# One GpSimd combination moved behind its addition into S, and four VectorE operations per turn made two, in a four-layer modulated convolution

## The chip, the cores and the metric

The kernel runs on one core of a Trainium2 chip. The metric is the time of one execution in device microseconds (us); the kernel before has a median of 495.83 us in three runs (495.58 to 497.23).

## The reference

For 128 samples of 64 channels by 1024 positions, the reference adds to x the result of four convolution layers of three taps, each with weights of its own for each sample:

```python
def _layer(x, style, w, b, mw, mb, typ):
    s = style @ mw.T + mb
    weight = SCALE * w * s[:, None, :, None]
    demod = lax.rsqrt(jnp.sum(weight * weight, axis=(2, 3)) + EPS)
    weight = weight * demod[:, :, None, None]
    ...            # 'same', 'upsample' (with a blur), 'same', 'downsample' (with a blur)
out = x
for i, typ in enumerate(('same', 'upsample', 'same', 'downsample')):
    out = _layer(out, style, weights[i], biases[i], mod_w[i], mod_b[i], typ)
return x + out
```

Nothing in it is nonlinear, so a sample's four layers are one linear filter away from the ends of the sequence, and the few positions at the ends are computed on their own.

## The kernel before, in words

Four samples make a group q, so there are 32 groups (NQ = 32), two pairs of two samples each. For each group the kernel composes the filter from the layers' weights and then convolves x with it. All of it is in float32.

The weights of a group come from a chain of small matmuls on TensorE with 64 x 64 tiles. `scale3` scales the last layer's taps, `stage1_a` and `stage1_b` multiply them with the third layer's into PSUM psS, from where they come to the tile S; `stage2` multiplies S with the blur and the second layer into psR, and `stage3` with the first layer into psW and from there into Wf. In `stage1_b` VectorE writes two sums into S (L422), and then an addition (L425) puts a third part of S together: `t[:, :, 2] + t[:, :, 0]`. The first matmul of `stage2` (L439) reads that part.

The convolution is a fast one in the manner of Toom and Cook: x is split into three planes, five combinations T0 to T4 of the planes are multiplied with five combinations of the taps, and the products are recombined. The combinations go over an intermediate tile G (one buffer):

- `in_g01` (L555, recorded at L501): two planes of G from x, one VectorE operation for each pair of samples (128 x 688)
- `in_g2` (L560, recorded at L501): the third plane of G, both pairs in one operation
- `in1` (L565) and `in2` (L570): T1 and T2 from G, the sum and the difference of two planes, both pairs in one operation of 128 x 684, on GpSimd in nearly every turn
- `in04` (L577): T0 and T4 from G, one VectorE operation for each pair
- `in3` (L550): T3 from x, on VectorE

`conv0` to `conv4` (L590) are the products on TensorE, in PSUM psA, and for `conv4` in Y. `sum1` (y) and `sum2` (Y, then y at L641) are VectorE's recombinations between them; they have one input in PSUM. `combine_a` and `combine_b` (H, L501, and L498) are VectorE's combinations of the taps. ScalarE copies and scales what leaves PSUM and writes the output; SP issues the loads and stores.

The order on each engine is the order of the program text: there is no planner, each engine runs its own instructions in the order in which the loop issues them and waits on semaphores. Turn q of the loop convolves with group q, prepares n = q + 1 further, composes the weights of c = q + 2 and begins those of s = q + 3. It opens with `stage2(c)`, the Y sum of `sum2(q)` and `conv4(q)`, and closes with `conv2(n)`.

Eleven turns are slot turns (q = 1, 2, 3, 5, 6, 7, 9, 12, 14, 19, 24): they carry one more group of small matmuls (`slot`), for the ends of the sequence and for constants, at the place where the others call `stage1_a`. So in a slot turn `stage1_a` comes later, and `stage1_b` behind the first third of `conv2`. `extra(q, 0)` and `extra(q, 1)` stand near the end of a turn, behind `stage1_b`, and give some turns up to q = 25 a few small operations on VectorE, GpSimd or ScalarE.

In the kernel before, GpSimd runs `in1(c)` and `in2(c)` one behind the other in each turn from q = 1. In turns without a slot it then runs the addition of `stage1_b(s)`. In slot turns that addition is VectorE's, by the argument `nc_v`:

```python
        if q and c < NQ - 1:
            in1(c, nc_g)
            in2(c, nc_g)
        ...
        if q in SLOTS:
            stage1_a(s)
        elif s < NQ:
            stage1_b(s)
        ...
        if q in SLOTS:
            stage1_b(s, nc_v)
        extra(q, 0)
        extra(q, 1)
```

Of the kernel before, what the change touches and what calls it, by code (L numbers as in the profile page):

```python
# [50 lines left out]
ALU = mybir.AluOpType  # L51
# [12 lines left out]
def kernel(  # L64
# [12 lines left out]
    NQ = B // 4  # L77
# [5 lines left out]
    nc_v, nc_a, nc_g = nc.vector, nc.scalar, nc.gpsimd  # L83
# [42 lines left out]
    PL = NXC // 3  # L126
# [239 lines left out]
    def tap_matmul(ps, wd, at, n, weight, taps, first=False, last=False):  # L366
        for r, rows in enumerate(HALF):
            for c, cols in enumerate(HALF):
                nc.tensor.matmul(  # L369
                    ps[r][cols, at * C : (at + n) * C],  # L370
                    weight[rows],
                    wd[c if r == 0 else 1 - c][rows, taps],
                    start=first,
                    stop=last,
                    skip_group_check=True,
                )
# [34 lines left out]
            scaled_copy(nc_a, flat(st[r][:, :4]), ps[r][:, : 4 * C], tBn[:, q, r : r + 1])  # L411
        chain[q] = wd, ps, st, t

    def stage1_b(q, eng=nc_g):

        wd, ps, st, t = chain[q]
        tap_matmul(ps, wd, 1, 1, w2n[:, 3, :], slice(3, 4))
        tap_matmul(ps, wd, 3, 1, w2n[:, 4, :], slice(4, 5), last=True)
        for r in range(2):
            p1 = st[r][:, 0:1, :].to_broadcast([P, 2, C])  # L420
            sums = ps[r][:, C : 5 * C].rearrange("c (a b o) -> c a b o", a=2, b=2)[:, :, 0]
            nc_v.scalar_tensor_tensor(  # L422
                st[r][:, 4:, :], sums, tB[:, q, r : r + 1], p1, op0=ALU.mult, op1=ALU.subtract
            )
        eng.tensor_add(t[:, :, 2], t[:, :, 2], t[:, :, 0])  # L425
        chain[q] = st

    def stage2(q, pool=None, engs=(nc_a, nc_a), between=None):
# [71 lines left out]
    def sum_of(out, x, f, y, op=ALU.add):  # L500
        nc_v.scalar_tensor_tensor(out, x, f, y, op0=ALU.mult, op1=op)  # L501
# [23 lines left out]
    NJ = NB + 2  # L525
# [2 lines left out]
    A = {}  # L528
    SLOT = {0: ("T04", 0), 4: ("T04", 1), 1: ("T12", 0), 2: ("T12", 1), 3: ("T3", 0)}
    BOTH_PAIRS = slice(0, 2)  # L530

    def plane(buf, i, pairs=BOTH_PAIRS):

        at = PL * (2 - i) if i < 3 else PL * 2 + 1
        return buf[:, pairs, at : at + NJ]

    def t_tile(q, tag):
        if (q, tag) not in Ts:
            Ts[q, tag] = tpool.tile([P, 2, 1 + (tag != "T3"), PL], F32, tag=tag, name=f"{tag}_{q}")
        return Ts[q, tag]  # L540

    def g_tile(q):
        if q not in Gs:
            Gs[q] = gpool.tile([P, 2, 3 * PL], F32, tag="G", name=f"G{q}")
        return Xs[q % NX], Gs[q]

    def in3(q, pairs=BOTH_PAIRS):
        if q < NQ:
            X, t = Xs[q % NX], t_tile(q, "T3")
            nc_v.tensor_sub(t[:, pairs, 0, :NJ], plane(X, 3, pairs), plane(X, 1, pairs))  # L550

    def in_g01(q, c):
        if q < NQ:
            X, g = g_tile(q)
            sum_of(g[:, c, PL:], X[:, c, : 2 * PL], 0.5, X[:, c, PL:], ALU.subtract)  # L555

    def in_g2(q, pairs=BOTH_PAIRS):
        if q < NQ:
            X, g = g_tile(q)
            sum_of(plane(g, 2, pairs), plane(X, 3, pairs), 0.5, plane(X, 2, pairs), ALU.subtract)  # L560
# [6 lines left out]
    def in2(q, eng):  # L567
        if q < NQ:
            t, g = t_tile(q, "T12"), Gs[q]
            eng.tensor_sub(t[:, :, 1, :NJ], plane(g, 2), plane(g, 1))  # L570

    def in04(q, c):
        if q < NQ:
            t, g = t_tile(q, "T04"), Gs[q]
            a, b = g[:, c, :NJ], g[:, c, 2 * PL : 2 * PL + NJ]
            both = lambda v, step: bass.AP(v.tensor, v.offset, [list(v.ap[0]), [step, 2], [1, NJ]])
            nc_v.tensor_sub(t[:, c, :, :NJ], both(a, PL), both(b, 1))  # L577

    def product(q, m, ps, groups=range(K)):

# [43 lines left out]
    def conv1(q, *groups):  # L624
        product(q, 1, banks(q), groups or range(K))
# [106 lines left out]
    def const_of(l, bs):  # L732

        n = bs.stop - bs.start
        at = NB + 4 + l * n
        return Y[:, 0, at : at + n]
# [4 lines left out]
    def const_first(l, bs):  # L741
        src = c0f if l == 0 else cc[l - 1]
        for cols in HALF:
            nc.tensor.matmul(
                const_of(l, bs)[cols],
                wsum[T, l, :],
                src[T, bs],
                start=False,
                stop=True,
                skip_group_check=True,  # L750
            )
# [218 lines left out]
    var_newton(PART[0])  # L970
    for of in (table_C, vector_c0, table_3, vector_a1, vector_Da, vector_b1, vector_c2):
        of(PART[0])
    in_g01(0, 0)
    in3(0)
    stage2(0, None, BOTH)
    psL = unit(ps_conv, "psL")
# [1 line left out]
    nc_a.copy(raw[0][:, 0, :n_later], psL[0][:, :n_later])  # L978
    zeros_to_y(2, 456)
    const_first(0, PART[0])  # L980
    in_g01(0, 1)
    in_g2(0)
    load(NX)
    split_weights()
# [10 lines left out]
    conv3(0)  # L995
    copy_m3(0)
    const_first(1, PART[0])
    in04(0, 0)
    in04(0, 1)
    const_rest(1, PART[0], const_of(1, PART[0]))  # L1000
    stage3(1, 0)
    mod_by_layer(LATER, raw[0][:, 0], sc, AF.Identity)
    in3(1)
    conv1(0)
    in_g01(1, 0)
    in_g01(1, 1)
    const_first(2, PART[0])
    sum1(0)
    const_rest(2, PART[0], const_of(2, PART[0]))
# [15 lines left out]
    n, n1 = (bs.stop - bs.start for bs in (REST, PART[1]))  # L1025
# [75 lines left out]
    for q in range(NQ):  # L1101
        n, c, s = q + 1, q + 2, q + 3
        if q == 1:
            nc.sync.dma_start(Xe, x_ends)
        if q == 5:
            zeros()
        if n == NQ:
            conv4(q)
            for i in range(2):
                output(q, 2, i)  # L1110
            for i in range(2):
                output(q, 1, i, nc_v)
            for i in range(2):
                store(q, i, slice(1, 3))
            conv0(q, *range(K))
            for i, (eng, queue) in enumerate(zip(BOTH, (nc_a, nc.sync))):
                output(q, 0, i, eng)
                store(q, i, slice(0, 1), queue)
            break
        if c < NQ:  # L1120
            stage2(c)
        if n < NQ - 1:
            sum2(q)
        if n < NQ - 1:
            combine_a(n)
            combine_b(n)

        if n == NQ - 1:

            conv3(n, ps_w)  # L1130
            copy_m3(n)
            conv4(q, 0, 1)
            for i in range(2):
                output(q, 1, i)
            conv1(n)
            sum1(n)
            conv4(q, 2)
            for i in range(2):
                output(q, 2, i)
            in04(n, 0)  # L1140
            in04(n, 1)
            conv0(q, 0)
            conv2(n)
            conv0(q, 1, 2)
            sum2(n)
            for i in range(2):
                output(q, 0, i)
                store(q, i)
            continue

        conv4(q)
        if q == 0:
            var_matmul(PART[1], var_of(PART[1]), start=False)
            var_root(PART[1], var_of(PART[1]))
            var_inverse(PART[1])
            var_newton(PART[1])
            table_A(PART[1], dm[:, 2, PART[1]])
            for of in (table_C, vector_c0, table_3, vector_Da):
                of(PART[1])
        for i in range(2):  # L1160
            output(q, 2, i)
        if c < NQ:
            stage3(c, 0)
        conv3(n)
        copy_m3(n)
        in04(n, 0)
        in04(n, 1)
        if q:
            in3(c)
            in_g01(c, 0)  # L1170
            in_g01(c, 1)
        if c < NQ:
            stage3(c, 1)
        conv0(q, 0)
        conv1(n, 0)
        if q in SLOTS:
            slot(*SLOTS[q])
        elif s < NQ:
            stage1_a(s)
        conv1(n, 1, 2)  # L1180
        for i in range(2):
            output(q, 1, i)
        if q:
            in_g2(c)
            load(c + NX)
        if q and c < NQ - 1:
            in1(c, nc_g)
            in2(c, nc_g)
        if n == NQ - 2:
            combine_a(n + 1, lambda: sum1(n))  # L1190
            combine_b(n + 1)
        else:
            sum1(n)
        if q == 0:
            in_g01(c, 0)
            in_g01(c, 1)
        conv0(q, 1)
        if q in SLOTS:
            stage1_a(s)
        elif s < NQ:  # L1200
            stage1_b(s)
        conv0(q, 2)
        for i in range(2):
            output(q, 0, i)
        conv2(n, 0)
        if q in SLOTS:
            stage1_b(s, nc_v)
        extra(q, 0)
        extra(q, 1)
        if s + 1 < NQ:  # L1210
            scale3(s + 1)
        conv2(n, 1, 2)
        if n == NQ - 2:
            sum2(n)
            in1(n + 1, nc_v)
            in2(n + 1, nc_v)
        if q == 0:
            in_g2(c)
            in3(c)
            load(c + NX)  # L1220
            in1(c, nc_g)
            in2(c, nc_g)
        for i in range(2):
            store(q, i)
# [74 lines left out]
```

## Time and profile before

| | |
|---|---|
| median of three runs | 495.83 us |
| the profiled execution's own time | 496.51 us |
| its span in the profile | 494.7 us |
| granted TensorE clock | 0.997 |
| VectorE steps for G (L501) | 96, of 866 ns |
| VectorE steps for T0 and T4 (L577) | 64, of 865 ns |
| GpSimd steps in1, in2 (L565, L570) | 30 of each, of 1669 and 1666 ns |
| additions into S (L425) | 18 on GpSimd, 11 on VectorE |

The profile names an engine PE (matmuls), PEld (weight loads, which run beside the matmuls), DVE (VectorE), ACT (ScalarE) or POOL (GpSimd). A row of the view of groups has the line, the engine, the operation, what is written from what, the count, and then the busy time, the mean length of one and the idle time of the engine ahead of it. A row of the waits has who waited for whom, the time in total, how often and the longest. A row of the timeline has the start and the length in us, both counted from the span's start, and in brackets the idle time ahead of it and who ended it. Rows of the timeline merge equal neighbours (x2, x24), and the window that was asked for cuts them off. One turn of the loop goes from one first load of psR to the next.

### The profile page before, as it was taken

The numbers are of one execution on the slowest core, as the hardware profiler recorded it, in microseconds if no ns is written. First come the engines' busy times: TensorE is split into PE (matmuls) and PEld (weight loads), VectorE is DVE, ScalarE is ACT, GpSimd is POOL, SyncE is SP. The second block draws the span as 40 slices with busy tenths as digits, with TensorE's granted clock in tenths as the row PEclk, the third lists the DMA queues.
The fourth block names the chain that finished last, engine by engine and source line by source line (L and its number), as shares of the span: only waits on it lengthen the run. The fifth ranks groups of instructions, "written<-read, shape, count | busy, mean of one in ns | idle before, by whom it ended". The sixth has DMA issues, their size and how long they took to land.

```text
span 494.7 us, 22227 instructions
## 1 busy us (share of the span) xinstructions
PE 481.8 (97%) x10056; PEld 355.1 (72%) x10056; DVE 398.7 (81%) x704; ACT 290.5 (59%) x579; POOL 137.0 (28%) x164
## 2 busy tenths in 40 slices
PE   8999999999999999999999999999999999999994
PEld 6877687767777766767777777766766777777752
DVE  4986888798898869997768897759998768878783
ACT  5456646556565656556566556656555657566552
POOL 3544412344213223121223112223123323211200
PEclk9999999999999999999999999999999999999998
DMA  7220744443334442344443334442344442434224
GB/s 248 94 90 4 237 155 168 173 167 113 109 133 173 174 171 93 102 158 170 173 154 108 114 145 173 174 164 75 115 166 173 173 173 89 160 128 161 89 86 170
DMA packets 19727, 70.42 MB, mean 142 GB/s; under 512 B 2224, under 2 KB 2992, under 8 KB 19632
## 3 DMA queue, kind: packets, MB, share of 16 engines
q1 hardware_dynamic: 19408, 68.70, 39.0%
q8 instruction: 79, 1.29, 1.0%
q10 hardware_dynamic: 224, 0.29, 0.2%
q14 instruction: 16, 0.13, 0.1%
HBM read 35.36 MB, written 33.62 MB: 139 GB/s over the span
## 4 chain that ended last, share of the span: by engine, by line
PE 82%; DVE 11%; POOL 4%; issue 2%; ACT 1%; POOLq 0%; DVEq 0%
PE psA L590 37%; PE psR L439 14%; PE psW L480 13%; PE Y L590 9%; PE psS L369 5%; DVE G L501 3%; PE psE L820 2%; DVE H L501 2%; POOL T L565 1%; DVE T L577 1%; POOL T L570 1%; PE Y L169 1%; DVE Y L501 1%; DVE y L641 1%; DVE Wf L498 1%
## 5 line engine op out<-in xcount | busy, mean ns | idle before, releaser
L590 PE MATMUL psA<-T,H 64*64 64x340 f32 x2304 | 192.2, 446 | 0.7 <-DVE y L501 0.7
L565 POOL TENSOR_TENSOR T<-G 128x684 f32<-128x684 f32 x30 | 50.1, 1669 | 306.7 <-DVE G L501 266.6
L590 PEld LDWEIGHTS psA<-T,H 64*64 64x64 f32 x2304 | 92.8, 133 | 53.0 <-issue 6.7
L439 PE MATMUL psR<-S,E 64*64 64x192 f32 (+1 forms) x2304 | 88.0, 301 | 3.6 <-POOL S L425 2.3
L439 PEld LDWEIGHTS psR<-S,E 64*64 64x64 f32 x2304 | 77.3, 133 | 18.0 <-POOL S L425 7.6
L340 ACT ACTIVATE R<-psR,tC 128x448 f32<-128x448 f32 x63 | 36.6, 631 | 75.7 <-PE psR L439 73.9
L501 DVE SCALAR_TENSOR_TENSOR G<-X 128x688 f32<-128x688 f32 (+1 forms) x96 | 78.1, 866 | 0.0
L590 PE MATMUL psA<-T,Wf 64*64 64x340 f32 x768 | 74.0, 447 | 0.0
L501 DVE SCALAR_TENSOR_TENSOR y<-psA,m 128x680 f32<-128x680 f32 (+1 forms) x33 | 27.8, 845 | 46.8 <-PE psA L590 46.6
L340 ACT ACTIVATE Wf<-psW,t 128x384 f32<-128x384 f32 (+1 forms) x126 | 56.4, 498 | 11.5 <-PE psW L480 11.5
L480 PE MATMUL psW<-R,w0s 64*64 64x128 f32 (+1 forms) x1536 | 62.1, 287 | 0.4 <-ACT Wf L340 0.3
L590 PE MATMUL Y<-T,Wf 64*64 64x340 f32 x768 | 61.6, 446 | 0.4 <-DVE Y L501 0.3
L480 PEld LDWEIGHTS psW<-R,w0s 64*64 64x64 f32 x1536 | 51.1, 133 | 8.2 <-ACT Wf L340 1.2
L577 DVE TENSOR_TENSOR T<-G 128x684 f32<-128x684 f32 x64 | 52.7, 865 | 0.0
L659 ACT ACTIVATE o<-Y,tb,td 128x340 f32<-128x340 f32 x64 | 37.2, 631 | 23.4 <-ACT R L340 16.8
L570 POOL TENSOR_TENSOR T<-G 128x684 f32<-128x684 f32 x30 | 50.0, 1666 | 0.0
L369 PEld LDWEIGHTS psS<-wd,w2n 64*64 64x64 f32 x1160 | 38.5, 133 | 11.1
L659 ACT ACTIVATE o<-psA,tb,td 128x340 f32<-128x340 f32 x63 | 36.7, 634 | 14.9 <-PE psA L590 14.9
L590 PEld LDWEIGHTS Y<-T,Wf 64*64 64x64 f32 x768 | 31.8, 133 | 17.0 <-DVE Y L501 1.0
L340 ACT ACTIVATE S<-psS,tBn 128x256 f32<-128x256 f32 x58 | 24.4, 471 | 25.4 <-PE psS L369 25.3
L622 ACT COPY m<-psA 128x680 f32<-128x680 f32 (+1 forms) x33 | 23.3, 710 | 25.4 <-PE psA L590 25.4
L659 ACT ACTIVATE o<-y,tb,td 128x340 f32<-128x340 f32 x62 | 38.1, 668 | 0.0
(148 smaller groups left out, 529.2 us busy)
## 6 DMA issues: line engine op xcount, KB each, us to landing
X<-in_x SPq DMA_DIRECT2D x64, 516.0 KB, 4.5
out<-o SPq DMA_DIRECT2D x62, 510.0 KB, 4.4
out<-o SPq DMA_DIRECT2D x2, 340.0 KB, 4.4
Xe<-in_x_ends SPq DMA_DIRECT2D x1, 512.0 KB, 7.4
par<-in_params SPq DMA_DIRECT2D x2, 192.0 KB, 3.5
par_s<-in_params_s SPq DMA_DIRECT2D x1, 196.0 KB, 2.8
par<-in_params SPq DMA_DIRECT2D x2, 96.0 KB, 2.9
out<-Oe SPq DMA_DIRECT2D x1, 192.0 KB, 1.9
```

What stands on the lines that cost most here:

```text
L340: nc_a.activation(dst, src, AF.Copy, scale=f)
L369: nc.tensor.matmul(ps[r][cols, at * C : (at + n) * C], weight[rows], wd[c if r == 0 else 1 - c][rows, taps], start=first, stop=last, skip_ ...
L439: nc.tensor.matmul(ps[r][cols, lo * C : (lo + m) * C], E[rows, e + 2, :], src[rows, a, :], start=(n == 0), stop=(n == 8), skip_group_check ...
L480: nc.tensor.matmul(ps[r][cols, at : at + m * C], w0s[kind][rows, k, :], rt[c][rows, first : first + K * (m - 1) + 1 : K, :], start=(n == 1 ...
L501: nc_v.scalar_tensor_tensor(out, x, f, y, op0=ALU.mult, op1=op)
L565: eng.tensor_add(t[:, :, 0, :NJ], plane(g, 2), plane(g, 1))
L570: eng.tensor_sub(t[:, :, 1, :NJ], plane(g, 2), plane(g, 1))
L577: nc_v.tensor_sub(t[:, c, :, :NJ], both(a, PL), both(b, 1))
L590: nc.tensor.matmul(ps[s][cols, :NB], w, Ts[q, tag][rows, c, i, g : g + NB], start=(g == 0 and m == 3), stop=(g == K - 1), skip_group_check ...
L622: nc_a.copy(m3c[q][:, s], a)
L659: nc_a.activation(dst, src, AF.Identity, bias=add, scale=d3)
L820: nc.tensor.matmul(ps[r][cols, : HB * n].rearrange("c (b j) -> c b j", j=n), weight(i, r, c)[rows], moving(i, r, c)[rows], start=(i == 0), ...
```

## The change

Three things are different. In every turn from q = 1, in2 is issued behind `stage1_b`, so that GpSimd has in1, the addition into S, and then in2. `stage1_b` has lost its engine argument, so the addition of the eleven slot turns is GpSimd's, too. And `in_g01` and `in04` take a slice of pairs: within the loop, both pairs go in one VectorE operation, as they did for `in_g2` and `in3`; for the first groups and for the last one the pairs stay apart.

```diff
-    def stage1_b(q, eng=nc_g):
+    def stage1_b(q):
...
-        eng.tensor_add(t[:, :, 2], t[:, :, 2], t[:, :, 0])
+        nc_g.tensor_add(t[:, :, 2], t[:, :, 2], t[:, :, 0])
...
+    PAIR = slice(0, 1), slice(1, 2)
...
-    def in_g01(q, c):
+    def in_g01(q, pairs=BOTH_PAIRS):
         if q < NQ:
             X, g = g_tile(q)
-            sum_of(g[:, c, PL:], X[:, c, : 2 * PL], 0.5, X[:, c, PL:], ALU.subtract)
+            sum_of(g[:, pairs, PL:], X[:, pairs, : 2 * PL], 0.5, X[:, pairs, PL:], ALU.subtract)
...
-    def in04(q, c):
+    def in04(q, pairs=BOTH_PAIRS):
         if q < NQ:
             t, g = t_tile(q, "T04"), Gs[q]
-            a, b = g[:, c, :NJ], g[:, c, 2 * PL : 2 * PL + NJ]
-            both = lambda v, step: bass.AP(v.tensor, v.offset, [list(v.ap[0]), [step, 2], [1, NJ]])
-            nc_v.tensor_sub(t[:, c, :, :NJ], both(a, PL), both(b, 1))
+            a, b = g[:, pairs, :NJ], g[:, pairs, 2 * PL : 2 * PL + NJ]
+            both = lambda v, step: bass.AP(
+                v.tensor, v.offset, [*(list(d) for d in v.ap[:-1]), [step, 2], [1, NJ]]
+            )
+            nc_v.tensor_sub(t[:, pairs, :, :NJ], both(a, PL), both(b, 1))
...
-        in04(n, 0)
-        in04(n, 1)
+        in04(n)
         if q:
             in3(c)
-            in_g01(c, 0)
-            in_g01(c, 1)
+            in_g01(c)
...
-        if q and c < NQ - 1:
+        later = q and c < NQ - 1
+        if later:
             in1(c, nc_g)
-            in2(c, nc_g)
...
         if q in SLOTS:
-            stage1_b(s, nc_v)
+            stage1_b(s)
+        if later:
+            in2(c, nc_g)
         extra(q, 0)
         extra(q, 1)
```

More of the change, by code (lines that the diff above doesn't have):

```diff
@@ L972 @@
         of(PART[0])
-    in_g01(0, 0)
+    in_g01(0, PAIR[0])
     in3(0)
@@ L980 @@
     const_first(0, PART[0])
-    in_g01(0, 1)
+    in_g01(0, PAIR[1])
     in_g2(0)
@@ L997 @@
     const_first(1, PART[0])
-    in04(0, 0)
-    in04(0, 1)
+    in04(0)
     const_rest(1, PART[0], const_of(1, PART[0]))
@@ L1004 @@
     conv1(0)
-    in_g01(1, 0)
-    in_g01(1, 1)
+    in_g01(1, PAIR[0])
+    in_g01(1, PAIR[1])
     const_first(2, PART[0])
@@ L1139 @@
                 output(q, 2, i)
-            in04(n, 0)
-            in04(n, 1)
+            in04(n, PAIR[0])
+            in04(n, PAIR[1])
             conv0(q, 0)
@@ L1165 @@
         copy_m3(n)
-        in04(n, 0)
-        in04(n, 1)
+        in04(n)
         if q:
             in3(c)
-            in_g01(c, 0)
-            in_g01(c, 1)
+            in_g01(c)
         if c < NQ:
@@ L1194 @@
         if q == 0:
-            in_g01(c, 0)
-            in_g01(c, 1)
+            in_g01(c)
         conv0(q, 1)
```

## The prediction

> **What bounds the kernel now.** I read the page's busy shares first, then the waits, then the timeline around each start of psR, the first matmul group of a loop turn.
>
> ```profile
> PE 481.8 (97%) x10056; PEld 355.1 (72%) x10056; DVE 398.7 (81%) x704; ACT 290.5 (59%) x579; POOL 137.0 (28%) x164
> ```
>
> TensorE is the bound. So VectorE work that vanishes is worth something only in turns where TensorE waits for it. Which waits does TensorE have?
>
> ```profile
> PEld psR L439 <- POOL S L425: 7.6, 11, 1.3
> ...
> PE psR L439 <- POOL S L425: 2.3, 4, 0.7
> ```
>
> Inside the loop they stand almost all at psR, which needs GpSimd's addition into S: eleven waits of the weight loads, 7.6 us, of which 2.3 us in four turns (q=4, 10, 20, 21) reach the matmuls. An ordinary turn, q=26 into 27:
>
> ```profile
> 431.07 0.87 DVE L501 SCALAR_TENSOR_TENSOR y<-psA,m 128x680 f32<-128x680 f32 x1 [1.56 <-PE psA L590]
> 431.31 1.65 POOL L570 TENSOR_TENSOR T<-G 128x684 f32<-128x684 f32 x1
> ...
> 431.86 0.60 DVE L422 SCALAR_TENSOR_TENSOR S<-psS,tB,S 128x128 f32<-128x128 f32 x2
> ...
> 432.92 0.45 POOL L425 TENSOR_TENSOR S<-S 128x128 f32<-128x128 f32 x1
> ...
> 433.55 2.64 PEld L439 LDWEIGHTS psR<-S,E 64*64 64x64 f32 x72
> ```
>
> S is ready on VectorE at 432.46, but the addition starts at 432.92, when in2 (L570) leaves GpSimd; it ends at 433.37 and psR starts at 433.55. Here nothing is lost. One of the four bad turns, q=10:
>
> ```profile
> 195.25 1.65 POOL L570 TENSOR_TENSOR T<-G 128x684 f32<-128x684 f32 x1
> 195.30 2.01 DVE L835 TENSOR_TENSOR Ye<-raw,a 128x384 f32<-128x384 f32 x1
> ...
> 196.85 0.77 POOL L425 TENSOR_TENSOR S<-S 128x128 f32<-128x128 f32 x1
> ...
> 197.67 0.21 PEld L439 LDWEIGHTS psR<-S,E 64*64 64x64 f32 x8 [1.31 <-POOL S L425]
> ```
>
> in2 is late, so the addition is late (it ends at 197.62) and psR starts 0.05 behind it. A second thing is to be seen: L835, 384 elements from SBUF and SBUF, takes 2.01 us beside in2, and the addition 0.77 instead of 0.45 beside L835. In the slot turn q=9, with GpSimd idle, the same L835 takes 0.56:
>
> ```profile
> 182.97 0.56 DVE L835 TENSOR_TENSOR Ye<-raw,a 128x384 f32<-128x384 f32 x1
> 183.56 0.56 DVE L836 TENSOR_TENSOR Ye<-Ye,c 128x384 f32<-128x384 f32 x1
> 184.03 0.86 DVE L501 SCALAR_TENSOR_TENSOR Y<-m,psA 128x680 f32<-128x680 f32 x1
> ```
>
> So a VectorE step with its inputs in SBUF and a GpSimd step exclude each other: L835 stood about 1.45 us, until in2 was done. The Trainium skill, "SBUF — State Buffer", section "SBUF: two separate sides", says that the two share a port pair under an exclusive lock, held for the whole instruction by whichever starts first. The trace agrees (0.56 against 2.01 us), and by that rule a long in2 hurts wherever such steps meet it.
>
> **The change part by part.** *In2 behind the addition, turns without a slot.* The addition then waits for S and in1 alone. S is ready 1.1 us before psR in the ordinary turn (432.46 to 433.55), so nothing is gained there. In the four bad turns the wait goes; at most 2.3 us of matmul time, or, were each load wait to count in full, 7.6. I take the lower, since in the slot turn below psR's loads wait 0.48 us and no idle time stands at its matmuls. Of these 2.3 I count 1.2. What is late next is VectorE: these turns have extra steps between S and the Y sum (L501, Y<-m,psA), in2 now stands in their middle instead of at their head, and conv4, whose loads follow psR's 2.64 us of loads at once, needs Y. For q=20 three such steps are left and I count nothing; for q=4 and 10 0.3 each; for q=21, whose two steps fit around the addition, 0.6.
>
> *The addition of the slot turns, from VectorE to GpSimd.* There are eleven (q = 1, 2, 3, 5, 6, 7, 9, 12, 14, 19, 24), and in each psR hangs directly on this addition. q=9:
>
> ```profile
> 181.63 0.61 DVE L422 SCALAR_TENSOR_TENSOR S<-psS,tB,S 128x128 f32<-128x128 f32 x2 [1.61 <-PE psS L369]
> ...
> 182.16 0.28 DVE L425 TENSOR_TENSOR S<-S 128x128 f32<-128x128 f32 x1
> ...
> 182.55 0.17 PEld L439 LDWEIGHTS psR<-S,E 64*64 64x64 f32 x3 [0.48 <-issue]
> ```
>
> S ends at 182.24, psR starts at 182.55: 0.31 us. On GpSimd there come the hand-over, the addition and the way to psR. The hand-over is read from in1, which starts at 429.69 when the third G step ends at 429.52:
>
> ```profile
> 427.08 2.44 DVE L501 SCALAR_TENSOR_TENSOR G<-X 128x688 f32<-128x688 f32 x3
> ...
> 429.69 1.66 POOL L565 TENSOR_TENSOR T<-G 128x684 f32<-128x684 f32 x1 [10.26 <-DVE G L501]
> ```
>
> That is 0.17 us. The addition's durations on both engines:
>
> ```profile
> L425 POOL TENSOR_TENSOR S<-S x18: 447/517/975, 43.8 to 461.1; 128x128 f32<-128x128 f32 x18
> L425 DVE TENSOR_TENSOR S<-S x11: 279/281/944, 62.1 to 405.1; 128x128 f32<-128x128 f32 x11
> ```
>
> 0.17 + 0.45 + 0.05 is 0.67 against 0.31: 0.36 us later, eleven times 4.0. Corrections, estimates from the spread of these two rows and the lengths of the steps beside them: the one addition of 0.94 us on VectorE (q=1, beside in2) gets better by 0.7 against that, q=5 and q=7, which now lose 0.15 and 0.27 to in2, too; q=7 and q=19 have a step of 0.7 at the head of their extras, which the addition must let pass (0.3 each), q=12 and 14 one of 0.4 (0.1 each). Sum 3.6 us. Bounds: 0 if something hides it (I see no cover: psR is the next group in TensorE's order), and 11 × (0.975 − 0.279 + 0.22) = 10 if each addition met a VectorE step.
>
> The addition on GpSimd now waits for S, and in2 is queued behind it, then the small tables of the extras. Conv2, which reads in2's result, stands at the end of the next turn, and the next G steps, which overwrite its input, start no more than 6.5 us ahead of the next psR (427.08 to 433.55), half a turn after in2 is over; the tables are read later still, and no DMA is issued from this queue. So I cost the later in2 at nothing on this side; if a slot turn's addition were late by half a turn, G would wait, and in1 and S behind it.
>
> *In2 beside VectorE's extras in slot turns.* Until now in2 was long over when these ran. Now it starts when the addition ends, about 0.65 us behind S, and holds 1.65 us. Y and y read PSUM and don't meet it: in the ordinary turn y ran 0.87 us with most of it beside in2, and its 680 elements cost no more than a G step's 688. But extras that are not done by then stand still, and Y is queued behind them. I let the engines take turns: one extra step before the addition, one before in2. Two extras get through (q=1, 5, 12, 14, 19, 24), more don't. q=6 has six:
>
> ```profile
> 136.81 0.28 DVE L425 TENSOR_TENSOR S<-S 128x128 f32<-128x128 f32 x1
> ...
> 137.59 0.26 DVE L238 SCALAR_TENSOR_TENSOR dm<-nw,dm 128x96 f32<-128x96 f32 x1
> ...
> 139.03 0.86 DVE L501 SCALAR_TENSOR_TENSOR Y<-m,psA 128x680 f32<-128x680 f32 x1
> ...
> 139.94 0.21 PEld L590 LDWEIGHTS Y<-T,Wf 64*64 64x64 f32 x8 [0.33 <-DVE Y L501]
> ```
>
> L236, as short as L238, moves to 136.81, where the addition was; the addition runs to 137.5, L237 to 137.7, in2 to 139.35, the other four (1.44 us, from 137.59 to 139.03) to 140.8. Y comes 1.76 later, and conv4 already waits for it: 1.4 us on top of psR's 0.36. q=9: its copies get through, in2 runs from 183.0 to 184.65, L835 and L836 are left (1.06, from 182.97 to 184.03) and perhaps a copy, Y starts at 185.8 instead of 184.03; conv4, due 2.64 behind psR at 185.19, now has 0.3 to spare on a Y that ends at 184.89: 1.1 on top. q=3 waits already:
>
> ```profile
> 95.66 0.21 PEld L590 LDWEIGHTS Y<-T,Wf 64*64 64x64 f32 x8 [0.66 <-DVE Y L501]
> ```
>
> Its reciprocal runs beside the addition, the rest stands: about 1.0. q=2 and q=7, with one short step left: 0.2 each. Sum 3.9; bounds 0 (VectorE wins the pair each time) and 5 × 1.65 = 8.
>
> *One operation for both pairs.* Some thirty turns lose two starts of a VectorE step.
>
> ```profile
> L501 DVE SCALAR_TENSOR_TENSOR G<-X 128x688 f32<-128x688 f32 (+1 forms) x96 | 78.1, 866 | 0.0
> ```
>
> Against the addition on VectorE (128 elements, 0.279) 560 elements more cost 0.587 us, so 688 alone are 0.72 us. In the row of three G steps above a further one costs (2.44 − 0.866) / 2 = 0.787. One start less is thus worth 0.07 us (bounds 0 and 0.866 − 0.72 = 0.15), 0.14 per turn, if the longer operation keeps its rate; the G step and the T0/T4 step (L577) of the two pairs write separate places as before. It counts where VectorE sets the pace, and I take four turns: −0.6, with bounds of 0 and 30 × 0.3 = 9. Elsewhere, as in the ordinary turn, VectorE stands idle 1.56 us ahead of y until TensorE is done with psA, and an earlier G step only lengthens that.
>
> **Sum.** +3.6 + 3.9 − 1.2 − 0.6 = +5.7 on the profiled execution's 496.51 us (of which 494.7 is the span): 502.2. That execution lies 0.68 above the median of 495.83; by the median it is 501.5.
>
> **The rivals.** *The lock costs nothing.* If VectorE gets its short steps through ahead of in2, what is left is 3.6 − 2.3 − 0.6 = +0.7: 496.5. For it: steps of 0.2 us find gaps easily. Against it: L835's 2.01.
>
> *Faster: the load waits count in full.* If psR's loads set TensorE's pace, then all 7.6 us come back at the eleven psR of turns without a slot, the slots lose 4.0, the merges give 0.6, and with no lock the time is 495.83 − 7.6 + 4.0 − 0.6 = 491.6. It decides from the point where a load wait under 0.5 us costs matmul time. For it: the loads' row of waits is three times that of the matmuls. Against it: 0.48 us of load wait without idle matmuls in q=9, and the lock would take its 3.9 back, which leaves 495.5.
>
> *The lock takes more.* in2 could also reach the H steps in each slot turn (it ends about 1.6 us behind psR, and H starts there): 0.3 in each of ten, and G and in1 after them: 502.2 + 3 = 505.2, by the median 504.5. Conv3 needs the H sums later, so I don't take it.
>
> **How the numbers follow.** Forecast as above, 498 to 504.5: 0.64. Lock without cost, 494.5 to 497: 0.12. Faster by the load waits, 491 to 494.3: 0.14. More than 504.5: 0.10. About 0.3% (1.5 us) is what a measurement here tells from no change. Slower 0.74, within 0.12, faster 0.14. Range 495.0 to 505.0, which leaves most of the fast rival out and a little above; the forecast's own range is 498 to 504.5.
>
> **What would show it.** Right: in slot turns psR about 0.67 us behind S, with "POOL S L425" as releaser; VectorE's extras stretched by about 1.65 us in q=3, 6, 9, and conv4 waiting for Y there; in turns without a slot the addition ahead of in2 and no wait at psR; merged steps near 0.279 + 1248 × 0.00105 = 1.59 us. Wrong: no longer waits for Y, or ordinary turns shorter than now from psR to psR, which would mean that the load waits counted.

## The result, and the profile after

The changed kernel takes 494.2 us, median of 15 runs (493.27 to 495.95); the kernel before, run beside it, 495.88 (495.18 to 497.23). The ratio is 0.9961, with an interval from 0.9951 to 0.9971: faster by 1.9 us by the ratio, by 1.7 between the medians. The forecast was 501.5 with a range from 495.0, so both its sign and its range were wrong. The profiled execution took 494.43 us with a span of 492.6, against 496.51 and 494.7 before. The lines of the code move: in1 is now L566, in2 L571, the T0/T4 step L580, the product L593, while L422, L425 and L439 keep their numbers.

The page of the changed kernel, busy shares and two of its groups:

```profile
PE 480.1 (97%) x10056; PEld 363.4 (74%) x10056; DVE 406.0 (82%) x632; ACT 290.3 (59%) x579; POOL 141.9 (29%) x175
...
L571 POOL TENSOR_TENSOR T<-G 128x684 f32<-128x684 f32 x30 | 53.2, 1775 | 0.0
L580 DVE TENSOR_TENSOR T<-G 128x1368 f32<-128x1368 f32 (+1 forms) x33 | 50.5, 1534 | 0.0
```

VectorE has 72 instructions fewer and is 7.3 us *busier* (398.7 to 406.0): "busy" holds the time in which it stands behind GpSimd (with the merged operations alone, in e1 below, it is 392.5). in2 too has become longer (1.775 us in the mean, 1.666 before). TensorE does the same 10056 matmuls in a shorter span. Now the waits of the changed kernel (total, times, longest):

```profile
POOL S L425 <- ACT S L340: 20.3, 11, 4.0
...
PEld Y L593 <- DVE Y L501: 6.0, 9, 1.1
...
PE Y L593 <- DVE Y L501: 2.8, 5, 0.8
```

The row "psR L439 <- POOL S L425" of before, 7.6 us of load waits, is gone altogether, in the slot turns too, where the prediction expected it to appear. At conv4 nine waits for Y have grown out of two; five of them reach the matmuls as idle time (2.8 us). The row at the top names the mistake: eleven times, in q=0 and in ten of the eleven slot turns (in q=1 in1 is late), GpSimd sat idle until **ScalarE** (L340) released the addition. The view of L425's own instructions says the same, and lists nobody who waits for them:

```profile
L425 POOL TENSOR_TENSOR S<-S x29: 448/459/474, 43.8 to 457.8; 128x128 f32<-128x128 f32 x29
its engine sat idle before it (us, times) until:
  ACT S L340: 20.3, 11
who waited for it (us, times):
```

The slot turn q=9 after, whose stretch of before stands in the prediction:

```profile
180.12 0.84 ACT L340 ACTIVATE S<-psS,tBn 128x256 f32<-128x256 f32 x2 [0.28 <-PE psS L369]
...
181.04 0.46 POOL L425 TENSOR_TENSOR S<-S 128x128 f32<-128x128 f32 x1 [2.52 <-ACT S L340]
...
181.46 1.65 POOL L571 TENSOR_TENSOR T<-G 128x684 f32<-128x684 f32 x1
...
181.58 0.61 DVE L422 SCALAR_TENSOR_TENSOR S<-psS,tB,S 128x128 f32<-128x128 f32 x2 [1.61 <-PE psS L369]
...
182.11 1.05 DVE L816 COPY a<-Da 64x64 f32<-64x64 f32 x1
182.15 2.62 PEld L439 LDWEIGHTS psR<-S,E 64*64 64x64 f32 x72
...
184.65 0.86 DVE L501 SCALAR_TENSOR_TENSOR Y<-m,psA 128x680 f32<-128x680 f32 x1
...
185.56 0.49 PEld L593 LDWEIGHTS Y<-T,Wf 64*64 64x64 f32 x12 [0.80 <-DVE Y L501]
```

The addition starts at 181.04, 0.08 us after ScalarE's two copies are done (180.12 to 180.96), and is over at 181.50, before VectorE's two sums (L422) have even begun. psR follows at 182.15 with no wait, a moment before the sums are through (182.19): its first matmuls read parts 1 to 3, and only the next ones the sums. In the kernel before, the addition stood behind these sums in VectorE's queue and psR came at 182.55. Measured from the start of the sums, psR started 0.92 us behind it before and 0.57 now.

The code says why. L411 lets ScalarE write parts 0 to 3 of S (`flat(st[r][:, :4])`). L425 adds part 0 to part 2 and reads nothing else. VectorE's sums at L422 write parts 4 and 5 (`st[r][:, 4:, :]`). So the addition never depended on the sums. In the kernel before it was late by the order of a queue alone: behind the sums on VectorE in slot turns, behind in2 on GpSimd in the others.

Where did the time go? From start and end of every matmul record I worked out how much later each group of the loop began than it could have (its idle time and 0.2 us, by which groups that wait for nothing overlap in the records). A loss at psR or conv4 is put down to the turn q whose addition or extras it waits for; both groups open turn q + 1. Summed over the loop, in the two profiled executions:

| us lost ahead of | before | after |
|---|---|---|
| psR, turns without a slot | 3.7 | 0 |
| psR, slot turns | 2.3 | 0 |
| conv4's first group (waits for Y) | 1.0 | 4.9 |
| other groups of the loop | 1.7 | 2.7 (0.73 of it one gap without a releaser) |

6.0 us come back at psR and 3.9 are handed over to conv4, the next group that needs a late engine. The 2.1 that are left fit the result. But the other groups lost 1.0 more in this execution, so the whole table falls by 1.1 only, and the loop, from the psR that opens q=0 to the one that opens q=29, is 1.4 us shorter (430.7 to 429.3). The same kernel profiled again (e14 below) lacks the gap of 0.73 us, and its loop is 1.8 shorter (428.9). A single profile is no better than that.

### The profile page after: what moved, and what is told of

Its sections match the earlier page's. It is cut to its first block, busy times and chain, and to the rows that moved or that the text cites. A ratio compares the mean times of both kernels' runs of the same rounds, so it can differ in the third digit from the quotient of the medians.

```text
span 492.6 us, 22188 instructions
## 1 busy us (share of the span) xinstructions
PE 480.1 (97%) x10056; PEld 363.4 (74%) x10056; DVE 406.0 (82%) x632; ACT 290.3 (59%) x579; POOL 141.9 (29%) x175
## 4 chain that ended last, share of the span: by engine, by line
PE 86%; DVE 9%; POOL 1%; issue 1%; ACT 1%; DVEq 0%
PE psA L593 40%; PE psW L480 14%; PE psR L439 12%; PE Y L593 11%; PE psS L369 5%; PE psE L823 2%; DVE Y L501 1%; DVE G L501 1%; PE Y L169 1%; DVE S L422 1%; ACT o L662 1%; DVE Ve L839 1%; PE Y L316 1%; DVE Ye L839 0%; DVE Ve L838 0%
## 5 line engine op out<-in xcount | busy, mean ns | idle before, releaser
L593 PE MATMUL psA<-T,H 64*64 64x340 f32 x2304 | 193.3, 446 | 0.6 <-DVE y L501 0.5
L593 PEld LDWEIGHTS psA<-T,H 64*64 64x64 f32 x2304 | 95.3, 133 | 51.1 <-issue 7.6
L566 POOL TENSOR_TENSOR T<-G 128x684 f32<-128x684 f32 x30 | 50.1, 1671 | 283.4 <-DVE G L501 251.5
L439 PE MATMUL psR<-S,E 64*64 64x192 f32 (+1 forms) x2304 | 87.6, 299 | 0.7 <-ACT S L340 0.4
L439 PEld LDWEIGHTS psR<-S,E 64*64 64x64 f32 x2304 | 80.8, 133 | 8.2 <-issue 1.0
L340 ACT ACTIVATE R<-psR,tC 128x448 f32<-128x448 f32 x63 | 36.6, 631 | 69.2 <-PE psR L439 67.4
L501 DVE SCALAR_TENSOR_TENSOR G<-X 128x1376 f32<-128x1376 f32 (+2 forms) x66 | 76.1, 1191 | 0.0
L593 PE MATMUL psA<-T,Wf 64*64 64x340 f32 x768 | 74.8, 447 | 0.0
L593 PE MATMUL Y<-T,Wf 64*64 64x340 f32 x768 | 62.2, 448 | 3.1 <-DVE Y L501 2.8
L340 ACT ACTIVATE Wf<-psW,t 128x384 f32<-128x384 f32 (+1 forms) x126 | 56.4, 498 | 12.2 <-PE psW L480 12.2
L571 POOL TENSOR_TENSOR T<-G 128x684 f32<-128x684 f32 x30 | 53.2, 1775 | 0.0
L580 DVE TENSOR_TENSOR T<-G 128x1368 f32<-128x1368 f32 (+1 forms) x33 | 50.5, 1534 | 0.0
L593 PEld LDWEIGHTS Y<-T,Wf 64*64 64x64 f32 x768 | 32.3, 133 | 20.9 <-DVE Y L501 6.0
L340 ACT ACTIVATE S<-psS,tBn 128x256 f32<-128x256 f32 x58 | 24.4, 471 | 25.7 <-PE psS L369 25.6
```

What stands on the lines that cost most here:

```text
L340: nc_a.activation(dst, src, AF.Copy, scale=f)
L439: nc.tensor.matmul(ps[r][cols, lo * C : (lo + m) * C], E[rows, e + 2, :], src[rows, a, :], start=(n == 0), stop=(n == 8), skip_group_check ...
L566: eng.tensor_add(t[:, :, 0, :NJ], plane(g, 2), plane(g, 1))
L580: nc_v.tensor_sub(t[:, pairs, :, :NJ], both(a, PL), both(b, 1))
L593: nc.tensor.matmul(ps[s][cols, :NB], w, Ts[q, tag][rows, c, i, g : g + NB], start=(g == 0 and m == 3), stop=(g == K - 1), skip_group_check ...
```

## The experiments

Two questions stand: which part of the change brings the 2 us, and is it true that the addition need not wait? The theory, A in the texts on record, is the one above: the addition needs ScalarE's copies only, its lateness was queue order, and what psR gains goes partly to conv4. Its rivals: that waits of the weight loads count in full, as one case of the prediction had it, and that VectorE's merged operations bring the gain. "On VectorE" and "on GpSimd" below speak of the addition. e1 to e4 start from the kernel before, all others from the changed kernel. Each run stands beside runs of the kernel before on the same occasion; kernels of different occasions are compared by their ratios to it, with the 95% interval in brackets. The sums of idle time are worked out as above, from one execution each.

**e1: the merged operations alone.** The kernel before with the merged G and T0/T4 steps.

```diff
-            in_g01(c, 0)
-            in_g01(c, 1)
+            in_g01(c)
```

> The merged G and T0/T4 operations alone, on the kernel before. Theory A (the addition into S reads only what ScalarE wrote, and the change frees psR from two queue orders): at most 0.6 us faster than before, 495.3 to 496, with psR's waits of before still there. Theory B (the gain comes from the shorter VectorE work): all of it, about 494.2. Theory C (the prediction: the addition waits for VectorE's sums, the slot turns lose by it): 0.6 us faster, 495.3.

495.19 us against 496.09 beside it: 0.999 (0.9978 to 1.0002), not told apart from no change. psR still lost 4.7 us. The interval leaves the merges 1.1 us at most, and e3 below has the whole gain without them.

**e2: the slot turns' addition on GpSimd, alone.**

```diff
-            stage1_b(s, nc_v)
+            stage1_b(s)
```

> The addition of the slot turns on GpSimd alone; in2 stays directly behind in1, no merged operations. Theory A: the eleven psR of slot turns start without waiting, some 2.0 to 2.3 us faster, 493.6 to 493.9, and no lock cost, since in2 is over before the extras. Theory B: no change, 495.9. Theory C: 0.36 us slower per slot turn, 3.6 in all, 499.5.

495.91 against 496.09: 0.9996 (0.9987 to 1.0005). Theory A missed here. The many small losses of slot turns, 0.07 to 0.14 each, went; but in2 still stood ahead of the addition in GpSimd's queue, and q=1, 5 and 7 lost 0.96, 0.45 and 1.01 instead of 0.79, 0.28 and 0.40. The timeline of this kernel in q=7:

```profile
150.56 1.64 POOL L570 TENSOR_TENSOR T<-G 128x684 f32<-128x684 f32 x1
...
151.81 0.94 DVE L800 TENSOR_TENSOR Xm<-Xe,sc 128x512 f32<-128x512 f32 x1
152.15 0.91 POOL L425 TENSOR_TENSOR S<-S 128x128 f32<-128x128 f32 x1
...
153.11 0.91 PEld L439 LDWEIGHTS psR<-S,E 64*64 64x64 f32 x28 [1.39 <-POOL S L425]
```

in2 ends at 152.20, an extra of VectorE (L800) has taken its place by then, and the addition takes 0.91 us instead of 0.46. The theory had the right dependency and forgot what else could stand ahead.

**e3: in2 behind the addition, alone.** The addition stays on VectorE in slot turns, so there in2 follows in1 at once.

```diff
             in1(c, nc_g)
-            in2(c, nc_g)
...
             stage1_b(s, nc_v)
+        if q and c < NQ - 1:
+            in2(c, nc_g)
```

> in2 behind the addition alone; the slot turns' addition stays on VectorE, so in2 follows in1 at once there. Theory A: the four bad psR waits of turns without a slot go (3.7 us of matmul time), and conv4 behind q=4, 10 and 20 gives 1.8 back to in2's lock: 1.9 us faster, 494.0. Theory B: no change. Theory C: 1.2 us faster, 494.7.

494.03 against 496.09: 0.9961 (0.9945 to 0.9977), the whole gain of the change. The load waits of this kernel at psR and conv4:

```profile
PEld psR L439 <- issue: 4.1, 9, 0.5
...
PEld psR L439 <- PE psA L590: 2.6, 3, 1.1
PEld Y L590 <- DVE Y L501: 2.1, 5, 0.7
```

No wait of psR for GpSimd is left. 2.4 us are still lost at psR, all in slot turns; conv4 loses 1.6. All 7.6 us of load waits for the addition went and the time fell by 2, so the rival by which they count in full is out.

**e4: the addition ahead of the sums.** The kernel before, with the order inside one step turned round; VectorE still adds in slot turns.

```diff
         wd, ps, st, t = chain[q]
+        eng.tensor_add(t[:, :, 2], t[:, :, 2], t[:, :, 0])
         tap_matmul(ps, wd, 1, 1, w2n[:, 3, :], slice(3, 4))
...
-        eng.tensor_add(t[:, :, 2], t[:, :, 2], t[:, :, 0])
```

> The kernel before with the addition issued ahead of the two sums of stage1_b, in slot turns still on VectorE. Theory A: the addition never needed the sums, so the slot turns' psR is free of them: 2.0 us faster, about 493.9. Theory B and C: no change, 495.9.

495.89 against 496.09: 0.9998 (0.9989 to 1.0006), again no gain where A expected one. Its load waits:

```profile
PEld psR L439 <- POOL S L417: 6.7, 10, 1.2
...
PEld psR L439 <- DVE S L423: 2.1, 3, 0.9
```

The slot turns' small losses went, which shows once more that the addition needs no sum. But in turns without a slot it still stood behind in2 (first row), and in q=5 and q=7 it met in2 on VectorE, which held it and the sums behind it (second row; 0.53 and 0.56 lost). Queue order inside one engine is not enough while in2 runs at that time. By the same count psR lost 4.0 us in this profile instead of 6.0, and conv4 some 0.3 to 0.6 more; why the times show nothing of the difference stays open.

**e5: the addition made to wait for the sums.** The changed kernel with a small copy ahead of the addition: to a scratch tile, two elements of each partition, one from part 4 of each half of S, which the two sums write.

```diff
+        nc_g.tensor_copy(seen, t[:, :, 4:5, 0:1])
         nc_g.tensor_add(t[:, :, 2], t[:, :, 2], t[:, :, 0])
```

> The changed kernel with a small GpSimd copy of two elements per partition of VectorE's sums ahead of the addition, so that the addition does wait for the sums, as the prediction had it. Theory A: in slot turns psR then starts 0.17 (hand-over) + 0.25 (the copy) + 0.45 + 0.05 = 0.9 us behind the sums instead of with them: 8 to 10 us slower than the changed kernel, 502 to 504. Theory C: it waits already, no more than the copy's 0.25 us in each slot turn, 2.7 us, 497.

503.34 against 495.93: 1.016 (1.0145 to 1.0176), slower by 7.4 us. This is the kernel that the prediction priced at +5.7, with the copies on top. By the count of idle time psR lost 7.4 us in slot turns (2.3 before) and conv4 4.6 (1.0 before). The slot turn q=9 of this kernel:

```profile
185.97 0.61 DVE L424 SCALAR_TENSOR_TENSOR S<-psS,tB,S 128x128 f32<-128x128 f32 x2 [1.61 <-PE psS L369]
...
186.71 0.19 POOL L427 COPY seen<-S 128x2 f32<-128x2 f32 x1 [3.77 <-DVE S L424]
...
186.85 0.45 POOL L428 TENSOR_TENSOR S<-S 128x128 f32<-128x128 f32 x1
...
187.36 2.38 PEld L442 LDWEIGHTS psR<-S,E 64*64 64x64 f32 x72 [0.95 <-POOL S L428]
187.36 2.73 PE L442 MATMUL psR<-S,E 64*64 64x192 f32 x72 [0.35 <-POOL S L428]
187.37 1.95 DVE L841 TENSOR_TENSOR Ye<-raw,a 128x384 f32<-128x384 f32 x1
```

S ends at 186.58 and psR starts 0.78 later: 0.13 for the hand-over, 0.14 until the copy lets the addition start, 0.45 for the addition and 0.06 to psR. Without the copy that is the prediction's 0.67 to within 0.03. psR's matmuls stand 0.35 us. L841 stands 1.95 us beside in2, as the prediction had it for the third step of its extras. With its copies, this one wait is worth some 9 us (503.34 against 494.2). The size of +5.7 is not confirmed by it: the copies take 2.5 us ahead of the eleven slot additions (0.14 to 0.54 each), and 2.0 are lost in q=0, whose addition now waits for its sums, too; neither is in the prediction's sum. What e5 shows is the sign: with the dependency that the prediction assumed, the change is a loss.

**e6 to e8: can the 3.9 us at conv4 be had too?** Three kernels from the changed one. e6 puts in2 back ahead of the addition in slot turns only; e7 issues the extras of q of 8 and more one turn later, behind the H sums; e8 does both.

```diff
             in1(c, nc_g)
+            if q in SLOTS:
+                in2(c, nc_g)
...
-        if later:
+        if later and q not in SLOTS:
             in2(c, nc_g)
```

> The changed kernel with in2 directly behind in1 in slot turns alone, where the addition comes much later anyway. Theory A: in2 no longer meets VectorE's extras there, and conv4's waits behind q=3, 5, 6, 9 and 19 go or shrink to what they were before: 2.1 us faster than the changed kernel, 492.1. Theory B: no change, 494.2.

```diff
-        extra(q, 0)
-        extra(q, 1)
+        if q < 8:
+            extra(q, 0)
+            extra(q, 1)
...
             combine_a(n)
             combine_b(n)
+        if q > 8:
+            extra(q - 1, 0)
+            extra(q - 1, 1)
```

> The changed kernel with the extras of turns q=8 and later issued in the next turn, behind the H sums, so that Y no longer stands behind them and in2 is over when they run. Theory A: conv4's waits behind q=9, 10, 19 and 20 go, 1.8 us faster than the changed kernel, 492.4. If VectorE's total work sets the pace there, no change, 494.2.

> The changed kernel with both: in2 early in slot turns, extras from q=8 later. Theory A: of some 4.7 us at conv4, what is left is q=4's 0.9 and what q=3 and q=6 had before: 2.9 us faster than the changed kernel, 491.3. Theory B: 494.2.

493.77, 493.88 and 493.66 us against 495.93: 0.9953 (0.994 to 0.9965), 0.9957 (0.9946 to 0.9969) and 0.9958 (0.9947 to 0.997). All three missed: none is told apart from the changed kernel. In e6 conv4 loses 2.2 instead of 4.9, but psR gets 2.3 back (q=1, 5 and 7: the addition is behind in2 again, as in e2). In e7 the waits of conv4 in q=9, 10, 19 and 20 are gone (3.1 left), and the loop of its profiled execution is 1.7 us shorter, but its time is 0.3 lower; the stretches outside the loop were longer by 1.2 in that execution. From profile to profile the start-up varied between 30.8 and 33.8 us and the tail between 31.7 and 32.8, which is as much as these edits are worth.

**e9 to e12: the slot half and the merges in company.** D in these texts holds that the slot half of the change is worth nothing net. e9 is the changed kernel with the slot addition back on VectorE (e3 and the merges). e10 is e9 with the extras later, as in e7. e11 is e10 with VectorE's addition ahead of its sums, as in e4. e12 is the changed kernel without the merges.

```diff
-            stage1_b(s)
+            stage1_b(s, nc_v)
```

> The changed kernel with the slot turns' addition given back to VectorE; in2 behind the addition elsewhere and the merged operations stay. Theory D (the gain is in2's place in turns without a slot, and the slot turns' addition on GpSimd wins some 2.4 us at psR only to lose 2.1 us at conv4 behind the extras that in2 then holds up): within 0.5 us of the changed kernel, or 0.5 to 1 us faster, 493.2 to 494.2. Theory E (the addition on GpSimd pays in company with the other two parts): 1.5 to 2 us slower than the changed kernel, 496.

> As e9, with the extras of q=8 and later issued in the next turn behind the H sums. Theory D: conv4 behind q=10 and 20 stops waiting (0.66 us in the run with in2 moved alone), 492.6 to 493.5. Theory E: 495.3.

> As e10, with VectorE's addition of slot turns issued ahead of the two sums. Theory D: psR's waits in slot turns of 0.07 to 0.14 us each go (1.1 us in all), those that stem from in2's lock stay: 491.5 to 493. Theory E: 495.

```diff
-            in_g01(c)
+            in_g01(c, PAIR[0])
+            in_g01(c, PAIR[1])
...
-        in04(n)
+        in04(n, PAIR[0])
+        in04(n, PAIR[1])
```

> The changed kernel with each pair's G and T0/T4 operation apart again. Theory D: the merged operations are worth what they were alone, 0.9 us, so 495.1. If they count for nothing once psR is free: 494.2.

Against 496.61 us: e9 494.48, 0.9951 (0.9933 to 0.9969); e10 494.35, 0.9959 (0.9941 to 0.9978); e11 492.5, 0.9909 (0.9891 to 0.9927); e12 493.32, 0.9935 (0.9915 to 0.9954). e9 is not told apart from the changed kernel: moving the slot addition takes 2.4 us away at psR and puts 2.8 on conv4 (2.1 there in e9, 4.9 after), as D has it. e10 missed: the later extras, expected to bring it to 492.6 to 493.5, show no gain. e12 came out below both of its expected times. **e11 has the lowest time of the study**: its interval lies below those of e9, e10 and the changed kernel (0.9951 to 0.9971), but meets e12's, and it was run on one occasion only. Its load waits at the two places:

```profile
PEld Y L593 <- DVE Y L501: 2.0, 3, 1.1
PEld psR L439 <- DVE S L423: 1.6, 2, 0.8
```

By its trace in2 follows in1 in slot turns and is over before most extras, the addition is early by queue order, and GpSimd is out of VectorE's way: 0.8 us lost at psR (q=5 and 7), 1.9 at conv4.

**e13 to e15: is e12 better than the changed kernel?** e13 is e11 without the merges, e14 the changed kernel once more, e15 is e12 once more, all beside one another.

> e11 with each pair's G and T0/T4 operation apart again. If the merged operations are worth nothing because in2 then comes ahead of VectorE's second small step in turn q=4 (as the trace of e12 against the changed kernel shows), this is as fast as e11, ratio 0.990 to 0.992, with conv4's wait behind q=4 (0.9 us in e11) gone and some other waits back. If they are worth their 0.6 to 0.9 us, ratio 0.993.

> The changed kernel once more, on one chip with e13 and e15: ratio 0.996.

> e12 once more, beside the changed kernel. If the merges are worth nothing in company: no slower than e14, ratio 0.994 to 0.996. If they are worth 0.9 us: ratio 0.998.

Against 496.65 us: e13 494.0, 0.9943 (0.9923 to 0.9962); e14 494.32, 0.9955 (0.9938 to 0.9972); e15 493.67, 0.9941 (0.9924 to 0.9957). e13 fits neither of its expectations (0.990 to 0.992, or 0.993). The intervals of e14 and e15 overlap: beside the moved in2 the merges bring nothing that can be measured, in either direction. Whether they help in e11 stays open, since e11 and e13 were compared on different occasions and their intervals meet (0.9927 and 0.9923).

The traces show one turn in which the merges cost time. q=4 of the changed kernel, then of e12 (VectorE's rows in the first fence of each, GpSimd's in the second):

```profile
105.48 2.08 DVE L268 TENSOR_TENSOR tA<-sc,dm 64x48 f32<-64x48 f32 x2
...
109.45 0.86 DVE L501 SCALAR_TENSOR_TENSOR Y<-m,psA 128x680 f32<-128x680 f32 x1
```

```profile
105.83 1.68 POOL L571 TENSOR_TENSOR T<-G 128x684 f32<-128x684 f32 x1
```

```profile
105.69 0.60 DVE L268 TENSOR_TENSOR tA<-sc,dm 64x48 f32<-64x48 f32 x2
...
107.11 0.93 DVE L236 TENSOR_TENSOR nw<-dm,var 128x192 f32<-128x192 f32 x1
...
108.75 0.86 DVE L501 SCALAR_TENSOR_TENSOR Y<-m,psA 128x680 f32<-128x680 f32 x1
```

```profile
106.19 1.64 POOL L571 TENSOR_TENSOR T<-G 128x684 f32<-128x684 f32 x1
```

With the merges G, and so in1 and in2, come 0.36 us earlier. in2 then starts ahead of the second of two small steps (L268), and the pair takes 2.08 us instead of 0.60. Without them in2 meets the extras only after the reciprocal (L230, 0.75 us in both kernels); L236 takes 0.93 instead of 0.36, and Y comes 0.70 sooner; conv4 loses 0.94 us behind this turn of the changed kernel and nothing in e12; e14 (0.90) and e15 (nothing) repeat it. A faster step moved a transfer of the lock to a worse place.

## Why the prediction was wrong, step by step

**What bounds the kernel.** Right: TensorE, with its waits inside the loop at psR. The loss was undersized: 2.3 us by the matmuls' row of waits, 6.0 by the turns. That row counts idle time only, and a group that starts on time overlaps the one before by 0.2 us, so each of the four waits cost 0.2 more (3.1 together); smaller losses, such as 0.40 in q=7, hardly show as idle time at all.

**In2 behind the addition, turns without a slot.** Right in kind: the wait went, conv4 was late next in q=4, 10 and 20, and q=21 lost nothing. Counted −1.2 net; by the trace 3.7 came back and 1.8 was handed over, −1.9. By the measured times e3, which is this step alone, is worth 1.9 (496.09 × 0.0039).

**The slot turns' addition, the step that failed.** "The addition then waits for S and in1 alone", "in each psR hangs directly on this addition", hence +3.6. psR did need the addition, but the addition did not wait for all of S. It read two parts that ScalarE had finished at 181.01 in q=9 of before, 1.54 us ahead of psR:

```profile
180.17 0.84 ACT L340 ACTIVATE S<-psS,tBn 128x256 f32<-128x256 f32 x2 [0.28 <-PE psS L369]
```

The hand-over of 0.17 from VectorE was priced for a dependency that does not exist. Instead of +3.6 this step gave −2.3 at psR, beside the moved in2; alone, in e2, it took away the small losses of 0.07 to 0.14 and made three others larger. The profile of before held the hint, one line of its waits (the addition of q=0, the only one of before that found GpSimd free):

```profile
POOL S L425 <- ACT S L340: 2.1, 1, 2.1
```

e5 confirms the direction: with the wait built in, the kernel is 7.4 us slower than before, though some 4.5 of that lie in the copies and in q=0, so that about 3 are left of the +5.7 (an estimate by subtraction). And the lower bound of that step, 0, was wrong as well: a step that leaves a queue can come *earlier* than before, and a gain was nowhere in its range.

**in2 beside VectorE's extras.** Right mechanism, over-sized: +3.9 for slot turns, against 2.2 by the trace (q=3 0.2, q=5 0.2, q=6 0.8, q=9 0.7, q=19 0.3; what conv4 lost there less what it lost before; q=5 and q=19 were counted as free). q=6 of the changed kernel:

```profile
135.41 0.46 POOL L425 TENSOR_TENSOR S<-S 128x128 f32<-128x128 f32 x1 [0.37 <-ACT S L340]
...
135.82 1.65 POOL L571 TENSOR_TENSOR T<-G 128x684 f32<-128x684 f32 x1
...
136.48 1.11 DVE L236 TENSOR_TENSOR nw<-dm,var 128x96 f32<-128x96 f32 x1
...
140.26 0.78 PEld L593 LDWEIGHTS Y<-T,Wf 64*64 64x64 f32 x16 [1.14 <-DVE Y L501]
```

The lock is there, but in2 starts 0.13 us ahead of VectorE's sums instead of well behind them, so 0.7 of its 1.65 us is over before the first extra starts. The sums, which have an input in PSUM, are not held up: in q=9 they take 0.61 us beside in2, as in the kernel before with GpSimd idle. The first extra takes 1.11 us instead of 0.26. The failed step thus fed this one: an early addition also made in2 early. The rule quoted in the prediction from the Trainium skill ("SBUF — State Buffer", section "SBUF: two separate sides"), that whoever starts first holds the lock for its whole instruction, agrees with these rows: L236 ends at 137.59, 0.12 us behind in2's end at 137.47.

**One operation for both pairs.** The merged step's length was right: 1.59 predicted; the merged T0/T4 steps take 1.577 us and the merged G steps 1.583 (the 1.534 of the row further up also holds two unmerged ones). Its −0.6 is within e1's interval (ratio 0.9978 to 1.0002), and in company no gain was seen (e14 and e15).

**The sum.** −1.9, −2.3, +2.2 and 0 make −2.0, where the prediction had +5.7; of the 7.7 between them the slot addition is 5.9. The profiled span fell by 2.1 and the median by 1.7; that the sum meets them so closely is in part luck, as the losses of the other groups show. The measured 494.2 lies among the times of the prediction's fast rival (491 to 494.3), but not for its reason: e3 removed 7.6 us of load waits and gained 2.

## What to carry to other kernels

Before you price a step that changes its engine or its place, read which *parts* of a tile it takes and who writes them; a step that is late may be late by its queue alone, and the releaser of the one instance that found its engine idle tells you which input it truly waits for last. Give each moved step a bound on the side of a gain as well, unless its data are shown to be late. And expect the next late input to take back part of what one wait gives: here two thirds of the time won ahead of psR came up again at conv4.

## What the runs showed that was not expected

In these rows, what a VectorE step lost to GpSimd went by when it started and not by its length. In q=9 after, a copy of 64 elements (L816) took 1.05 us, against 0.18 before. In q=10 after, the lock changed hands twice (VectorE's rows first, then GpSimd's):

```profile
195.79 0.81 DVE L838 TENSOR_TENSOR Ye<-raw,a 128x384 f32<-128x384 f32 x1
196.64 1.89 DVE L839 TENSOR_TENSOR Ye<-Ye,c 128x384 f32<-128x384 f32 x1
```

```profile
196.14 1.97 POOL L571 TENSOR_TENSOR T<-G 128x684 f32<-128x684 f32 x1
```

L838 (0.56 alone) stood until the addition was done at 196.19; in2 then stood until L838 was done at 196.60 and took 1.97 instead of 1.65; L839 stood until in2 was done at 198.11. So the engine that waits got the pair at the other's next boundary, twice running.

Single profiles hold gaps with no releaser. The changed kernel's has one of 0.73 us among the first matmuls of psW behind q=1; the profiles of e3 and of e14, the same kernel again, lack it, and those of e7, e12, e13 and e15 have 0.4 to 0.5 there. Where they come from stays open, and with the spread of the start-up (30.8 to 33.8 us) it is why single executions here settle nothing under 1 us.
